# A mixture-of-experts layer on one core: layer 3's cross terms, its gives and the W3 split behind layer 2's second near bank

## The chip, the cores and the metric

The kernel runs on one core of one Trainium2 chip. The metric is the device time of one execution in microseconds (us); lower is better. Engines: PE (TensorE, matmuls; PEld its weight loads), DVE (VectorE), ACT (ScalarE), POOL (GpSimd) and SP (SyncE, DMA issue).

## The reference

Each of 64 x 64 = 4096 tokens has 256 features. A gate picks two of eight experts for a token; each expert is a network of three layers (256 to 512 to 512 to 256), and the two results, weighted, are added to the token.

```python
gate = xn @ wg_W + wg_b + (genre_embed @ gg_W + gg_b)      # xn: x, RMS-normed
gate_w = softmax(gate); topk_w, topk_i = top_k(gate_w, 2)
cw = sum(one_hot(topk_i, 8) * topk_w[..., None])           # 8 weights, 6 of them 0
h1 = relu(einsum('bsh,ehm->bsem', x, W1) + b1)
h2 = relu(einsum('bsem,emn->bsen', h1, W2) + b2)
out_e = einsum('bsen,enh->bseh', h2, W3) + b3
return x + einsum('bseh,bse->bsh', out_e, cw)
```

## The kernel before

The tokens are routed on the chip: each expert's tokens are gathered into tiles of up to 128, run through the three layers, and added back to their rows in DRAM. The first part of the tokens gives the units 0 to 5 (one tile each, plain fp32 matmuls) while the routing of the rest is computed. From unit F = 6 a unit has 2 to 4 tiles of one expert, up to 512 tokens wide, and `row(u)` writes one unit. Which of 40 shapes the rest has is known at run time; a switch jumps to the code of that shape. In the execution profiled there are units 6 to 24, in groups of two or three units of one expert: 6-8, 9-11, 12-14, 15-16, 17-18, 19-20, 21-22, 23-24. Their widths are 384 columns but for 8 (480), 9 (352), 12 (312), 15 (504), 16 (512), 18 (400), 21 (344) and 24 (320).

In these units each fp32 operand is split into a high and a low part (`h`, `l`) and their spread (`d`), on ACT (high) and DVE (low, spread), and each product is taken in two passes:

- `near(u, l, n)`: high x high and low x low into PSUM bank n (0 to 3), line 1100, and then ACT scales the bank in place and adds the bias (line 1108). One call is a "near bank": 8 matmuls in layer 2, 4 in layer 1.
- `cross(u, l, n)`: the spreads' product is added to the same bank (line 1115), and then ACT writes the ReLU's high part (`h1h`, line 1124, or `h2h`, 1127) and DVE the low part (`h1l`, `h2l`, 1140).

Layer 3 of unit u - 1 runs inside `row(u)`. `near3` (1189) sums high and low products into banks 5 and 6, `scale3` (DVE, 1203) scales them in place and adds the bias, `cross3` (1209) adds the spreads' product, and `give` (ACT, 1232) multiplies each tile's rows with the token's weight into a buffer `ysE` or `ysO`, from which POOL adds them to the rows in DRAM (line 1251, an indirect DMA that must find the adds of the unit before landed). `spans` (1085) make `h1d` and `h2d`.

The last unit of a group also splits the next expert's weights: W1 (`high_w` on ACT as `w1h`, `low_w` and `span_w` on DVE), then W2 in two halves (`w2h`, line 1039, two ACT instructions of 1.05 us). The first unit of a group splits its W3 (`w3h` on ACT, `w3l` on DVE). `split_rows` (ACT `xh`, line 1075; DVE `xl`, 1076) splits the next unit's tokens.

The order on each engine is the order in which the code is written (`tc.manual_schedule()`): each engine takes its instructions in this order and waits on semaphores where data is not ready. In a unit PE's order is: four near banks and four cross banks of layer 1, `near3`, the first near bank of layer 2, `cross3`, three near banks, four cross banks.

Of the kernel before, what the change touches and what calls it, by code (L numbers as in the profile page):

```python
# [68 lines left out]
def kernel(  # L69
# [92 lines left out]
    w1l = [wall.tile([P, HC, M], F32R, name=f"w1{a}") for a in "hld"]  # L162
# [609 lines left out]
    ww, ex, cgs = {}, {}, {}  # L772
# [36 lines left out]
    def width(u):  # L809
        return BT if u < F else WQ * plan[u - F][1]  # L810
# [4 lines left out]
    def follow(u):  # L815
        return u > F and group(u) == group(u - 1)

    def size(u):
        return (width(u) + BT - 1) // BT
# [48 lines left out]
    def gather_cw(u):  # L868
        for k, b in enumerate(tiles(u)):
            cg = cgs[b] = cgR[:, u % NCG, k]  # L870
            fetch(cg, (cwdA if b < F else cwdR)[:, :], b)
# [27 lines left out]
    def transpose_x(u, which=None):  # L899
        bs, w, s0 = tiles(u), len(tiles(u)), slots(u).start  # L900
        if u > F:
            for k in range(w) if which is None else which:
                V.transpose(
                    xT[:, :, s0 + k, :].rearrange("p c (b k) -> p k c b", b=SQ),
                    shs[:, s0 + k].rearrange("p k (a c) -> p k c a", a=SQ),
                )
            return
        tp = PB[4][:, 0 : HC * BT].rearrange("p (c t) -> p c t", c=HC)
        g = ring(run, [P, H], "xg", 3, bs[0]).rearrange("p (r c) -> p c r", c=HC)
        for c in range(HC):  # L910
            nc.tensor.transpose(tp[:, c], g[:, c], ident)
        nc.scalar.copy(xT[:, :, s0, :], tp)
# [38 lines left out]
    def streams(u, end):  # L951
        q = mybir.EngineType.SP
        if F < u + 1 < end and not follow(u + 1):
            stream_3(u + 1, q)
        if F < u + 2 < end and not follow(u + 2):
            stream_1(u + 2, q)
            stream_2(u + 2, q)

    def stage_1(u):

        if u < F:
            ww[u] = [w1r[u % RING], vT[:, :, u, :], w2r[u % RING], w3r[u % RING]]
            return
        if follow(u):
            ex[u] = ex[u - 1]
            ww[u] = ww[u - 1][0:4]
            return
        e = ex[u] = expert(u, mybir.EngineType.DVE)
        bb = ring(run, [P, 2, MC], "bb", 3, group(u))
        V.tensor_copy(bb.unsqueeze(2), vT[:, :, e])  # L970
        k = group(u) % RING
        ww[u] = [w1r[k], bb, w2r[k], w3r[k]]

    def scales(u):

        n = size(u)
        cw = ring(run, [P, SLOTS], "cw", 3, u)
        V.tensor_copy(cw[:, 0:n].unsqueeze(2), cgR[:, u % NCG, 0:n, ex[u]])
        for k, b in enumerate(tiles(u)):
            cgs[b] = cw[:, k : k + 1]  # L980

    def scaled(u, eng="V"):
        for _ in scaling(u, eng):
            pass
# [50 lines left out]
    def plain(t):  # L1035
        return t.bitcast(F32)

    def high_w(dst, src):
        nc.scalar.activation(dst[0], src, AF.Copy, scale=NEAR * FINE)

    def low_w(dst, src):
        V.scalar_tensor_tensor(dst[1], plain(dst[0]), -1.0 / FINE, src, ALU.mult, ALU.add)

    def span_w(dst):
        V.tensor_tensor(dst[2], plain(dst[0]), plain(dst[1]), ALU.subtract)
# [16 lines left out]
    def w2_of(u, n, m):  # L1062
        cs = slice(n * P, m * P)
        return [t[:, :, cs] for t in room["w2"]], ww[u][2][:, :, cs]
# [17 lines left out]
    def spans(t3, u):  # L1082

        h, l, d = (t[:, :, 0 : width(u)] for t in t3)
        V.scalar_tensor_tensor(d, plain(l), 1.0 / FINE, plain(h), ALU.mult, ALU.subtract)  # L1085

    def fine(u, last):

        return u >= F and size(u) > 1 and u + 1 < last
# [4 lines left out]
    def near(u, l, n):  # L1094

        ws, xs = (w1l, xl) if l == 0 else (room["w2"], room["h1"])
        bank, k = PB[n][:, 0 : width(u)], HC if l == 0 else MC
        for c in range(k):
            for t in (0, 1):
                nc.tensor.matmul(  # L1100
                    bank,
                    lhsT=ws[t][:, c, ts(n, P)],
                    rhs=xs[t][:, c, 0 : width(u)],
                    start=c == 0 and t == 0,
                    stop=c == k - 1 and t == 1,
                    skip_group_check=True,
                )
        nc.scalar.activation(bank, bank, AF.Identity, bias=ww[u][1][:, l, n : n + 1], scale=1.0 + 1.0 / FINE)  # L1108
# [89 lines left out]
    def scale3(u):  # L1198
        row = b3_sb[:, ex.pop(u)]
        for k in range(0, size(u), 2):  # L1200
            n = min(2, size(u) - k)
            two = PB[5 + k // 2][:, 0 : n * H].rearrange("p (k h) -> p k h", k=n)
            V.scalar_tensor_tensor(two, two, 1.0 + 1.0 / FINE, row.to_broadcast([P, n, H]), ALU.mult, ALU.add)
# [41 lines left out]
    def pay():  # L1245
        adds.append([])
        add_rows(*owed.pop(0))
# [93 lines left out]
    def fetches_of(u, last):  # L1341
        far = F + 1 < u + 2 < last
        if far:
            gather_unit(u + 2)
            stow(u + 2)
        return far
# [26 lines left out]
    def row(u, last):  # L1373

        streams(u, last)
        far = fetches_of(u, last)
        if u == F:
            gather_cw(F)
            pay()
        follows = u + 1 < last  # L1380
        fresh_next = follows and not follow(u + 1)
        if follows:
            gather_cw(u + 1)
        n3, limbs = size(u - 1), fine(u - 1, last)
        fresh = u > F and not follow(u)
        if u == F + 1:
            scales(F)
        third = fine(u, last) and not (follow(u) and fine(u - 1, last))
        if third and not limbs:
            high_w(room["w3"], ww[u][3])  # L1390
        for n in range(MC):
            near(u, 0, n)
        if limbs:
            spans(room["h2"], u - 1)
            if not follow(u - 1):
                span_w(room["w3"])
        if fresh and not limbs:
            for n in (0, 2):
                span_w(w2_of(u, n, n + 2)[0])
        if third and not limbs:  # L1400
            low_w(room["w3"], ww[u][3])
        if follows and u > F:
            stage_1(u + 1)
            if u > F + 1 and not (fresh and limbs):
                transpose_x(u + 1)
        for n in range(MC):
            cross(u, 0, n)
        if fresh_next:
            high_w(w1l, ww[u + 1][0])
        if limbs:  # L1410
            near3(u - 1)
            if fresh and follows:
                transpose_x(u + 1, (0, 1))
            scale3(u - 1)
            if fresh and follows:
                transpose_x(u + 1, range(2, size(u + 1)))
        else:
            scaled(u - 1, "A")
            layer3(u - 1)
        if u == F:  # L1420
            split_w(*w2_of(u, 2, 4))
            stage_1(u + 1)
        if u == F + 1:
            transpose_x(u + 1)
        if fresh and limbs:
            for n in (0, 2):
                span_w(w2_of(u, n, n + 2)[0])
        spans(room["h1"], u)
        if u == F:
            transpose_x(u + 1)  # L1430
        else:
            scales(u)
        if far:
            shuffle(u + 2)
        near(u, 1, 0)
        if limbs:
            cross3(u - 1)
        give(u - 1)
        if third and limbs:
            high_w(room["w3"], ww[u][3])  # L1440
            low_w(room["w3"], ww[u][3])
        if fresh_next:
            low_w(w1l, ww[u + 1][0])
            span_w(w1l)
        near(u, 1, 1)
        if u == F:
            near(u, 1, 2)
            near(u, 1, 3)
        if follows:
            split_rows(u + 1)  # L1450
        elif not fine(u, last):
            scaled(u, "A")
        if fresh_next:
            high_w(*w2_of(u + 1, 0, 2))
            low_w(*w2_of(u + 1, 0, 2))
        if u > F:
            near(u, 1, 2)
            near(u, 1, 3)
        if fresh_next:
            high_w(*w2_of(u + 1, 2, 4))  # L1460
        for n in range(MC):
            cross(u, 1, n)
            if n == MC - 1 and follows:
                span_rows(u + 1)
            if n == 2 and hints:
                hints.pop()()
        if fresh_next:
            low_w(*w2_of(u + 1, 2, 4))
# [103 lines left out]
```

## Time and profile before

| | |
|---|---|
| time, median of 3 runs | 419.32 us (419.04 to 419.55) |
| the profiled execution: its own time, its span | 422.99 us, 421.3 us |
| granted TensorE clock in it | 0.997 |
| PE, PEld, DVE, ACT, POOL busy | 97%, 91%, 84%, 62%, 73% of the span |
| units 6 to 24 | from 74.6 us to the end; the last matmul starts at about 415 us |

A profile is one execution, and every duration below is from it. A line of a timeline gives the start, the duration, the engine and source line, output<-inputs, the shapes, how many instructions are merged ("x3"), and in brackets the idle time before them and what ended it. A line of a group gives its instructions' busy time and mean, and behind the second bar the idle time before them and its releasers. Matmuls overlap and their ends are modelled, so distances between matmuls are taken from start to start: 0.17 us at 384 columns, 0.12 us at 256.

### The profile page before, as it was taken

The page shows a single profiled execution, that of the slowest core. Times are in us where ns is not written, and L with a number is a line of the kernel's source. Part 1 is how long each engine was busy: PE and PEld are TensorE (multiplying, and loading weights), DVE is VectorE, ACT ScalarE, POOL GpSimd, SP SyncE. Part 2 cuts the span into 40 slices and gives each one's busy share as a digit, 9 for nine tenths or more (in the row PEclk, how much of TensorE's full clock was granted, in tenths as well). Part 3 has the DMA queues.
Part 4 walks back from the last instruction along what each step waited for, and adds up shares of the span by engine and source line. Part 5 has one row for each costly group of instructions (what it writes and reads, how often), then busy time and mean ns, then how long its engine had stood idle before and what let it go on. Part 6 is the DMA issues. An engine that isn't in the chain of part 4 may idle for free.

```text
span 421.3 us, 7909 instructions
## 1 busy us (share of the span) xinstructions
PE 408.8 (97%) x2664; PEld 385.1 (91%) x2664; DVE 351.9 (84%) x613; ACT 262.4 (62%) x536; POOL 306.8 (73%) x239
## 2 busy tenths in 40 slices
PE   8999999999999999999999999999999999999994
PEld 6788999799989999999999889899999989999992
DVE  5887986898879987899598979799988979989931
ACT  5965635764765748658468565748566575675750
POOL 6257347768888888878778888888788787874544
PEclk9999999999999999999999999999999999999998
DMA  8899996898735666538557663927386385550323
GB/s 309 304 331 386 379 370 185 232 260 248 165 76 112 177 161 150 115 87 228 140 141 208 158 125 91 259 71 136 93 240 148 76 212 160 106 105 8 39 29 44
DMA packets 72052, 72.31 MB, mean 172 GB/s; under 512 B 36191, under 2 KB 59074, under 8 KB 71620
## 3 DMA queue, kind: packets, MB, share of 16 engines
q1 hardware_dynamic: 56640, 54.04, 39.5%
q0 software_dynamic: 15008, 17.68, 23.5%
q8 instruction: 22, 0.36, 0.4%
q14 instruction: 26, 0.21, 0.2%
q10 hardware_dynamic: 356, 0.01, 0.0%
HBM read 55.86 MB, written 20.47 MB: 181 GB/s over the span
## 4 chain that ended last, share of the span: by engine, by line
PE 79%; DVE 5%; issue 5%; DMA 3%; POOL 3%; POOLq 2%; ACT 1%; SPq 0%; DVEq 0%; ACTq 0%
PE pb L1100 34%; PE pb L1115 16%; PE pb L1189 11%; PE pb L1209 6%; PE pb L1026 4%; DMA big<-in_x_dram 3%; PE pb L1014 2%; PE pb L1176 2%; POOL out_dram L1251 2%; POOLq L1487 1%; PE pb L272 1%; POOL cg L846 1%; DMA out_dram<-ysO,idxR 1%; PE pb L646 1%; DVE h2l L1140 1%
## 5 line engine op out<-in xcount | busy, mean ns | idle before, releaser
L1108 ACT ACTIVATE pb<-pb,bb 128x384 f32<-128x384 f32 (+8 forms) x152 | 84.8, 560 | 96.0 <-PE pb L1100 77.5
L1100 PE MATMUL pb<-h1h,w2h 128*128 128x384 f32 (+8 forms) x304 | 102.8, 340 | 0.0
L1100 PE MATMUL pb<-h1l,w2l 128*128 128x384 f32 (+8 forms) x304 | 102.8, 340 | 0.0
L846 POOL DMA_INDIRECT cg<-cwdR,idxR x61 | 77.6, 1272 | 18.6 <-issue 16.5
L1251 POOL DMA_INDIRECT out_dram<-ysE,idxR x30 | 58.9, 1962 | 16.2 <-ACT ysE L1232 8.9
L1251 POOL DMA_INDIRECT out_dram<-ysO,idxR x28 | 47.6, 1702 | 18.5 <-ACT ysO L1232 11.5
L1100 PEld LDWEIGHTS pb<-h1l,w2l 128*128 128x128 f32 x304 | 57.2, 188 | 2.3 <-DVE h1l L1140 0.2
L1100 PEld LDWEIGHTS pb<-h1h,w2h 128*128 128x128 f32 x304 | 57.2, 188 | 1.6
L1115 PE MATMUL pb<-h1d,w2d 128*128 128x384 f32 (+8 forms) x304 | 57.2, 339 | 0.2 <-ACT pb L1108 0.2
L1140 DVE SCALAR_TENSOR_TENSOR h2l<-pb,h2h 128x384 fp32r<-128x384 f32 (+7 forms) x72 | 39.2, 567 | 21.0 <-ACT h2h L1127 13.9
L1189 PE MATMUL pb<-w3l,h2l 128*128 128x256 f32 (+5 forms) x232 | 56.1, 282 | 0.0
L1189 PE MATMUL pb<-w3h,h2h 128*128 128x256 f32 (+5 forms) x232 | 56.1, 282 | 0.0
L1115 PEld LDWEIGHTS pb<-h1d,w2d 128*128 128x128 f32 x304 | 52.4, 188 | 2.2 <-ACT pb L1108 0.5
L1100 PE MATMUL pb<-xh,w1h 128*128 128x384 f32 (+8 forms) x152 | 51.8, 343 | 1.1 <-DVE h2l L1140 0.8
L1100 PE MATMUL pb<-xl,w1l 128*128 128x384 f32 (+8 forms) x152 | 51.3, 339 | 0.0
L846 POOL DMA_INDIRECT xgE<-in_x_dram,idxR x33 | 43.4, 1315 | 10.1 <-issue 7.9
L846 POOL DMA_INDIRECT xgO<-in_x_dram,idxR x28 | 37.5, 1340 | 8.5 <-issue 8.2
L1189 PEld LDWEIGHTS pb<-w3l,h2l 128*128 128x128 f32 (+5 forms) x232 | 43.3, 187 | 0.2
L1189 PEld LDWEIGHTS pb<-w3h,h2h 128*128 128x128 f32 (+5 forms) x232 | 43.3, 187 | 0.2
L1127 ACT ACTIVATE h2h<-pb 128x384 fp32r<-128x384 f32 (+7 forms) x72 | 34.4, 503 | 9.3 <-PE pb L1115 8.0
L1140 DVE SCALAR_TENSOR_TENSOR h1l<-pb,h1h 128x384 fp32r<-128x384 f32 (+8 forms) x76 | 37.5, 555 | 0.9 <-ACT h1h L1124 0.9
L1085 DVE SCALAR_TENSOR_TENSOR h1d<-h1l,h1h 128x1536 fp32r<-128x1536 f32 (+8 forms) x19 | 33.8, 1781 | 0.0
(278 smaller groups left out, 799.8 us busy)
## 6 DMA issues: line engine op xcount, KB each, us to landing
w2r<-in_L_cond_W_dram SPq DMA_DIRECT2D x14, 1024.0 KB
w1r<-in_L_cond_W_dram SPq DMA_DIRECT2D x14, 512.0 KB
w3r<-in_L_cond_W_dram SPq DMA_DIRECT2D x14, 512.0 KB
gTs<-scr SPq DMA_DIRECT2D x13, 384.0 KB
out_dram<-in_x_dram SPq DMA_DIRECT2D x4, 768.0 KB
scr<-xgO SPq DMA_DIRECT2D x7, 384.0 KB
scr<-xgE SPq DMA_DIRECT2D x6, 384.0 KB
big<-in_x_dram SPq DMA_DIRECT2D x4, 512.0 KB
```

Source lines behind the costliest of these rows:

```text
L846: return nc.gpsimd.indirect_dma_start(out=dst, out_offset=None, in_=src, in_offset=bass.IndirectOffsetOnAxis(ap=index(b), axis=0), bounds_ ...
L1014: nc.tensor.matmul(ph, lhsT=w1[:, c, ts(m, P)], rhs=cols[:, c, :], start=(c == 0), stop=(c == HC - 1))
L1026: nc.tensor.matmul(ph, lhsT=w2[:, m, ts(n, P)], rhs=hid[0][:, m], start=(m == 0), stop=(m == MC - 1))
L1085: V.scalar_tensor_tensor(d, plain(l), 1.0 / FINE, plain(h), ALU.mult, ALU.subtract)
L1100: nc.tensor.matmul(bank, lhsT=ws[t][:, c, ts(n, P)], rhs=xs[t][:, c, 0 : width(u)], start=c == 0 and t == 0, stop=c == k - 1 and t == 1, s ...
L1108: nc.scalar.activation(bank, bank, AF.Identity, bias=ww[u][1][:, l, n : n + 1], scale=1.0 + 1.0 / FINE)
L1115: nc.tensor.matmul(bank, lhsT=ws[2][:, c, ts(n, P)], rhs=xs[2][:, c, 0 : width(u)], start=False, stop=c == k - 1, skip_group_check=True,)
L1127: nc.scalar.activation(room["h2"][0][:, n, 0 : width(u)], bank, AF.Relu, scale=NEAR)
L1140: V.scalar_tensor_tensor(l, PB[n][:, 0 : width(u)], 0.0, plain(h), ALU.max, ALU.subtract)
L1189: nc.tensor.matmul(sums(u, k)[0 : cols.stop - cols.start], lhsT=room["h2"][t][:, n, cols], rhs=room["w3"][t][:, n, :], start=n == 0 and t ...
L1209: nc.tensor.matmul(sums(u, k)[0 : cols.stop - cols.start], lhsT=room["h2"][2][:, n, cols], rhs=room["w3"][2][:, n, :], start=False, stop=n ...
L1251: add = nc.gpsimd.indirect_dma_start(out=orows, out_offset=bass.IndirectOffsetOnAxis(ap=index(b)[0 : y.shape[0]], axis=0), in_=y, in_offse ...
```

## The change

In `row(u)` the second near bank of layer 2 moves ahead of `cross3`, the gives and the split of W3. The split of the next W1 (`low_w`, `span_w`, on DVE) moves with it. Nothing is added or removed.

```diff
         near(u, 1, 0)
+        if fresh_next:
+            low_w(w1l, ww[u + 1][0])
+            span_w(w1l)
+        near(u, 1, 1)
         if limbs:
             cross3(u - 1)
         give(u - 1)
         if third and limbs:
             high_w(room["w3"], ww[u][3])
             low_w(room["w3"], ww[u][3])
-        if fresh_next:
-            low_w(w1l, ww[u + 1][0])
-            span_w(w1l)
-        near(u, 1, 1)
```

`limbs` holds where unit u - 1 is split (from u = 7), `third` in a group's first unit, `fresh_next` in its last.

On PE, in unit 8 (480 columns), banks 68, 69 and 70 are layer 2's first, second and third near bank, and 73 and 74 the banks of layer 3; the rows with - are where `cross3` stood, those with + where it stands now, with the second near bank between them:

```order
 L1100 MATMUL pb_68<-h1l,w2l 128x480
-L1209 MATMUL pb_73<-w3d,h2d 128x256 x8
-L1209 MATMUL pb_74<-w3d,h2d 128x256 x4
 L1100 MATMUL pb_69<-h1h,w2h 128x480
 L1100 MATMUL pb_69<-h1l,w2l 128x480
+L1209 MATMUL pb_73<-w3d,h2d 128x256 x8
+L1209 MATMUL pb_74<-w3d,h2d 128x256 x4
 L1100 MATMUL pb_70<-h1h,w2h 128x480
```

`cross3` stands 8 matmuls later, in every unit from 7 to 24.

On ACT, in unit 11, the last of its group (384 columns; `w2h` are the halves of the next expert's W2):

```order
 L1108 ACTIVATE pb_68<-pb_68,bb_934 128x384
+L1108 ACTIVATE pb_69<-pb_69,bb_934 128x384
 L1232 ACTIVATE ysE<-pb_73,cw_1300 128x256 x2
 L1232 ACTIVATE ysE<-pb_74,cw_1300 128x256
-L1108 ACTIVATE pb_69<-pb_69,bb_934 128x384
 L1075 ACTIVATE xh<-xT 128x2x312
 L1039 ACTIVATE w2h<-w2r_86 128x4x256
```

The second bank's scaling now precedes the three gives; `xh` follows them directly.

On ACT, in unit 12, the first of its group (312 columns):

```order
 L1108 ACTIVATE pb_68<-pb_68,bb_935 128x312
+L1108 ACTIVATE pb_69<-pb_69,bb_935 128x312
 L1232 ACTIVATE ysO<-pb_73,cw_1301 128x256 x2
 L1232 ACTIVATE ysO<-pb_74,cw_1301 128x256
 L1039 ACTIVATE w3h<-w3r_89 128x1024
-L1108 ACTIVATE pb_69<-pb_69,bb_935 128x312
 L1075 ACTIVATE xh<-xT 128x2x384
```

Here the W3 split goes behind the second bank's scaling too. On DVE, POOL and SP the order of these units is unchanged.

## The prediction

> **What bounds the kernel now.** I read the page's busy shares and chain first, then the groups by line and the waits of the weight loads, then the timelines of PE, VectorE (DVE), ScalarE (ACT) and POOL around layer 2's first near bank.
>
> ```profile
> PE 408.8 (97%) x2664; PEld 385.1 (91%) x2664; DVE 351.9 (84%) x613; ACT 262.4 (62%) x536; POOL 306.8 (73%) x239
> PE 79%; DVE 5%; issue 5%; DMA 3%; POOL 3%; POOLq 2%; ACT 1%; SPq 0%; DVEq 0%; ACTq 0%
> ```
>
> PE is busy for 97% of the span and makes 79% of the chain that ended last. The change moves no work from one engine to another, so what it can give is PE's idle time near the moved instructions.
>
> ```profile
> L1209 PE MATMUL pb<-w3d,h2d 128*128 128x256 f32 (+5 forms) x232 | 31.5, 286 | 1.2 <-issue 0.7 <-DVE pb L1203 0.4
> L1209 PEld LDWEIGHTS pb<-w3d,h2d 128*128 128x128 f32 (+5 forms) x232 | 28.8, 186 | 3.7 <-issue 2.0 <-DVE pb L1203 1.2
> ```
>
> L1209 is `cross3`. Its weight loads (PEld) stood 3.7 us idle, of which the row names 3.2: 2.0 "issue" and 1.2 for L1203, VectorE's `scale3`. The matmuls themselves show only 1.2, because the pipelined end of the matmul before covers the start of a wait. Matmul starts tell more. First a unit that waits, then one that does not (both PE):
>
> ```profile
> 153.46 0.39 PE L1100 MATMUL pb<-h1l,w2l 128*128 128x384 f32 x1
> 154.02 1.68 PE L1209 MATMUL pb<-w3d,h2d 128*128 128x256 f32 x12 [0.17 <-issue]
> 155.54 0.34 PE L1100 MATMUL pb<-h1h,w2h 128*128 128x384 f32 x1
> ...
> 402.44 0.31 PE L1100 MATMUL pb<-h1l,w2l 128*128 128x320 f32 x1
> 402.58 1.60 PE L1209 MATMUL pb<-w3d,h2d 128*128 128x256 f32 x12
> 404.02 0.31 PE L1100 MATMUL pb<-h1h,w2h 128*128 128x320 f32 x1
> ```
>
> In the first, `cross3` starts 0.56 us after the last near matmul, in the second 0.14; and it then takes 1.52 instead of 1.44 until the next group starts. So one wait costs PE about 0.5. VectorE's timeline says what is late:
>
> ```profile
> 151.43 1.92 DVE L1140 SCALAR_TENSOR_TENSOR h1l<-pb,h1h 128x384 fp32r<-128x384 f32 x4
> 153.28 1.02 DVE L1203 SCALAR_TENSOR_TENSOR pb<-pb,b_sb 128x512 f32<-128x512 f32 x2
> 154.21 1.73 DVE L1085 SCALAR_TENSOR_TENSOR h1d<-h1l,h1h 128x1536 fp32r<-128x1536 f32 x1
> 155.87 0.14 DVE L978 COPY cw<-cg 128x3 f32 x1
> 159.07 0.96 DVE L1076 TENSOR_TENSOR xl<-xT,xh 128x768 fp32r<-128x768 f32 x1 [3.06 <-ACT pb L1108]
> ```
>
> `scale3` follows four `h1l` on a queue without a gap; its first bank ends just before 154.02, where `cross3` starts. By 156.0 VectorE is idle, for 3.06 us. It is late at this one place and ahead after it.
>
> **The change part by part.** *The waits of `cross3`.* Behind the second near bank `cross3` comes one bank later, 1.39 us at 384 columns (eight steps of 0.17), far more than 0.5, so `scale3` is done. The second near bank needs nothing new: all four `h1l` were read by the first. What is late next is `h1d`, needed by layer 2's cross terms: it ends at 155.94, and those start four near banks and `cross3` after 152.2, past 159. The gain lies between 1.2 (the matmul row) and 3.7 (the weight loads' row). Starts as above agree with the upper end; I take 3.4.
>
> *ScalarE in a group's last unit.* There the next expert's W2 is split, and ACT is full to the end (ACT, then the two rows of DVE and PE that follow from it):
>
> ```profile
> 171.13 0.56 ACT L1108 ACTIVATE pb<-pb,bb 128x384 f32<-128x384 f32 x1 [2.60 <-PE pb L1100]
> 172.55 1.21 ACT L1232 ACTIVATE ysE<-pb,cw 128x256 f32<-128x256 f32 x3 [0.87 <-PE pb L1209]
> 173.95 0.56 ACT L1108 ACTIVATE pb<-pb,bb 128x384 f32<-128x384 f32 x1 [0.19 <-issue]
> 174.43 0.72 ACT L1075 ACTIVATE xh<-xT 128x624 fp32r<-128x624 f32 x1
> 175.04 1.05 ACT L1039 ACTIVATE w2h<-w2r 128x1024 fp32r<-128x1024 f32 x1
> 175.99 0.54 ACT L1108 ACTIVATE pb<-pb,bb 128x384 f32<-128x384 f32 x1
> 176.72 0.56 ACT L1108 ACTIVATE pb<-pb,bb 128x384 f32<-128x384 f32 x1 [0.19 <-PE pb L1100]
> 177.20 1.05 ACT L1039 ACTIVATE w2h<-w2r 128x1024 fp32r<-128x1024 f32 x1
> 178.15 1.24 ACT L1127 ACTIVATE h2h<-pb 128x384 fp32r<-128x384 f32 x3
> ...
> 178.66 1.98 DVE L1140 SCALAR_TENSOR_TENSOR h2l<-pb,h2h 128x384 fp32r<-128x384 f32 x4 [1.31 <-ACT w2h L1039]
> ...
> 179.30 0.39 PE L1100 MATMUL pb<-xh,w1h 128*128 128x312 f32 x1
> ```
>
> The next unit's first matmul at 179.30 overwrites bank 0, so it needs the first `h2l`, which (a quarter of 1.98 after 178.66) ended only 0.1 before: lateness on ACT here goes straight to PE. Until now the gives (L1232) ran while PE did the second near bank. Now they start 1.39 later, at 173.94, take 1.10 until the next can start, and `xh` goes from 174.43 to 175.04. From there the steps of these rows run on: `w2h` 175.65, L1108 176.60 and 177.07, against 176.72 now, where it waited for PE. That is 0.35 late. But this give started 1.6 after its `cross3`, others 1.2 (in the last unit 403.74, quoted below, against 402.58): with that 0.4 back nothing is late. So 0 to 0.45 (a wider `xh` adds 0.1) in each of the five last units of 384 or 400 columns, 0 to 2.3; units of 480 and 512 have near banks long enough to hide it. I take 0.2 each, 1.0, as the two starts are about equally common. In a group's first unit the split of W3 goes behind the gives in the same way, and no W2 split follows:
>
> ```profile
> 354.13 1.21 ACT L1232 ACTIVATE ysE<-pb,cw 128x256 f32<-128x256 f32 x3 [0.78 <-PE pb L1209]
> 355.22 1.07 ACT L1039 ACTIVATE w3h<-w3r 128x1024 fp32r<-128x1024 f32 x1
> ...
> 358.40 0.52 ACT L1108 ACTIVATE pb<-pb,bb 128x344 f32<-128x344 f32 x1 [0.53 <-PE pb L1100]
> ```
>
> Gives at 355.4 (a bank of 344 columns is 1.25), `w3h` at 356.5, `xh` at 357.4, then L1108 at 358.1 and 358.6: 0.2 late where ACT had 0.53 to spare, and made good by the `h2h` that follow. Nothing. `low_w`, `span_w` of W1 keep their place on VectorE, since neither near banks nor gives run there; SP's order stays too.
>
> The rule that speaks against the change is the Trainium skill's (TensorE: Matmul & The Clock Gate, Architectural detail): ScalarE's queue is a strict FIFO, so a give that waits holds all behind it. The rows agree: ACT's order stood through every wait above. By the rule alone, with no give starting early, the toll would be its upper end, 2.3, and the sum -0.6.
>
> *POOL.* The scatter-adds keep their order but wait for later gives. Inside the run they push the gathers behind them, whose rows VectorE transposes (L903); that never waits now:
>
> ```profile
> L903 DVE STREAM_TRANSPOSE xT<-gTs 128x256 f32<-128x256 f32 x58 | 31.4, 631 | 0.0
> ```
>
> The gathers run a unit ahead, so 1.4 is hidden there. At the end it shows:
>
> ```profile
> 403.74 1.21 ACT L1232 ACTIVATE ysO<-pb,cw 128x256 f32<-128x256 f32 x3 [0.46 <-PE pb L1209]
> ...
> 404.50 1.55 POOL L1251 DMA_INDIRECT out_dram<-ysO,idxR  x1 [8.82 <-ACT ysO L1232]
> ...
> 408.19 3.65 DMA out_dram<-ysO,idxR
> ...
> 411.82 0.48 DVE L1234 SCALAR_TENSOR_TENSOR xg<-pb,cw,bc 128x256 f32<-128x256 f32 x1 [7.92 <-PE pb L1176]
> ...
> 412.71 1.54 POOL L1251 DMA_INDIRECT out_dram<-xg,idxR  x1 [2.97 <-DVE xg L1234]
> 414.76 1.55 POOL L1251 DMA_INDIRECT out_dram<-xg,idxR  x1 [0.51 <-DVE xg L1234]
> 416.61 1.44 POOL L1251 DMA_INDIRECT out_dram<-xg,idxR  x1 [0.30 <-issue]
> ```
>
> The last three adds may start only when the three before have landed, now at 408.19 + 3.65 = 411.84, before their give ends at 412.30. In the last unit nothing waited, so its `cross3` moves by one near bank, 402.58 - 401.41 = 1.17, and the landing to 413.0. The first add then starts 0.4 later, at 413.4, the others at POOL's step of 1.85: the third at 417.1 instead of 416.61. That is 0.5 lost; from 0.2 (if the landing is quicker) to 0.8.
>
> *A stall of the profiled run.* In one last unit ACT stood 1.67 us before L1108, and PE paid later:
>
> ```profile
> 339.50 0.56 ACT L1108 ACTIVATE pb<-pb,bb 128x384 f32<-128x384 f32 x1 [1.67 <-PE pb L1100]
> ...
> 342.19 1.67 PE L1115 MATMUL pb<-h1d,w2d 128*128 128x384 f32 x8 [0.18 <-ACT pb L1108]
> 344.61 0.43 PE L1100 MATMUL pb<-xh,w1h 128*128 128x344 f32 x1 [0.76 <-DVE h2l L1140]
> ```
>
> The change puts that L1108 ahead of the gives; 0 to 0.9 (0.18 + 0.76) could go. I count 0, since nothing in the order explains the stall.
>
> **Sum**: -3.4 + 1.0 + 0.5 = -1.9 us. The profiled execution took 422.99 (span 421.3); the median of the runs is 419.32, 0.9% less, and I take the same microseconds off it: 417.4. Ends: -3.7 - 0.9 + 0.2 = -4.4, or 414.9, and -1.2 + 2.3 + 0.8 = +1.9, or 421.2.
>
> **Rivals.** *The whole gain* (0.17): gives start early everywhere and the stall goes with them: -3.4 - 0.9 + 0.5 = -3.8, 415.5. For it: three of the seven last units have 0.5 us waits whose removal leaves ACT time; against: the stall has no cause that the change touches.
>
> *The wait moves* (0.21): VectorE sets the pace of the waiting units, and what `cross3` no longer waits for is waited for at `h2l` or the next `h1l`. Then two thirds of 3.4 come back: -1.1 + 1.0 + 0.5 = +0.4, 419.7, no change. Against it stand the 3.06 us in which VectorE waited for ACT in such a unit.
>
> *Slower* (0.12): ACT's order. If gives and what follows are late by 0.9 instead of 0.2 in the five units, as after the 1.67 at 339.50, then -3.4 + 4.5 + 0.5 = +1.6, 420.9. It decides from (3.4 - 0.5 + 0.84) / 5 = 0.75 a unit, twice what the rows of 171 to 179 give at worst. The FIFO rule above is its ground.
>
> **How the numbers follow.** The forecast has 0.50, the rivals 0.17, 0.21 and 0.12. About 0.2%, or 0.84 us, is what can be told from no change here, 418.5 to 420.2. The forecast (416.5 to 418.6 by itself) and the whole gain make faster, less a little of the forecast's upper side: 0.66. The moved wait and that side make 0.23 for the same, the slow rival 0.11. The range from 415.3 to 419.7 leaves out the slow rival and a part of the whole gain.
>
> **What would show it.** Right: idle before L1209's weight loads under 0.5 us; gives starting after a second near bank; the first matmul of the units after a W2 split idle by 0.2 more; the last unit's adds 1.2 nearer to the final ones. Wrong: new idle of PE before L1115 or at a unit's first L1100 of over 2 us in sum, or waits of `cross3` that stay.

## The result and the profile after

The changed kernel took 421.31 us (median of 19 runs, 419.79 to 423.9) against 419.1 us before (19 runs, 418.26 to 421.76): ratio 1.0052, interval 1.0036 to 1.0067, so it is 0.5% slower. The prediction was 417.4, faster. The profiled execution took 421.01 us, its span is 419.3, its granted clock 0.991. Ratios here leave out runs in a slower state of the chip and are not the quotient of the two medians.

The waits of `cross3` are gone. The two rows of L1209 in the changed kernel, matmuls and weight loads, show next to no idle time (1.2 and 3.7 us before):

```profile
L1209 PE MATMUL pb<-w3d,h2d 128*128 128x256 f32 (+5 forms) x232 | 30.5, 282 | 0.0
L1209 PEld LDWEIGHTS pb<-w3d,h2d 128*128 128x128 f32 (+5 forms) x232 | 29.5, 185 | 0.3
```

A new wait stands in the page of the changed kernel: the busy line, the chain, the group of near matmuls, and the transposes, which never waited before.

```profile
PE 407.0 (97%) x2664; PEld 386.6 (92%) x2664; DVE 351.2 (84%) x613; ACT 261.9 (62%) x536; POOL 314.8 (75%) x239
...
PE 81%; DVE 6%; DMA 5%; issue 3%; ACT 2%; POOL 1%; POOLq 1%; SPq 0%; DVEq 0%; ACTq 0%
...
L1100 PE MATMUL pb<-h1h,w2h 128*128 128x384 f32 (+8 forms) x304 | 104.0, 344 | 2.4 <-DVE h1l L1140 2.4
...
L903 DVE STREAM_TRANSPOSE xT<-gTs 128x256 f32<-128x256 f32 x58 | 31.3, 629 | 3.3 <-DMA gTs<-scr 3.3
```

All of it is in one place. PE's timeline of the changed kernel at unit 14 (start, duration; the last matmul of `near3`, then layer 2's first near bank), and below it the same time in stretches (length, busy time of PE, PEld, DVE, ACT and POOL, then the granted clock, DMA share and GB/s):

```profile
214.53 0.28 PE L1189 MATMUL pb<-w3l,h2l 128*128 128x256 f32 x1
217.24 0.69 PE L1100 MATMUL pb<-h1h,w2h 128*128 128x384 f32 x1 [2.43 <-DVE h1l L1140]
217.73 0.53 PE L1100 MATMUL pb<-h1l,w2l 128*128 128x384 f32 x1
218.05 0.53 PE L1100 MATMUL pb<-h1h,w2h 128*128 128x384 f32 x1
```

```profile
208.00:217.00 9.00, 6.81 (x47) 6.61 (x45) 5.60 (x10) 5.06 (x10) 7.47 (x6) 1.00 0.91 212
217.00:219.00 2.00, 1.76 (x5) 1.76 (x6) 2.00 (x5) 0.00 (x0) 1.39 (x3) 0.50 0.26 78
219.00:222.00 3.00, 3.00 (x16) 3.00 (x16) 3.00 (x5) 0.80 (x2) 2.70 (x2) 0.77 0.40 97
```

From start to start 2.71 us pass instead of 0.12: a gap of 2.59. Behind it the clock is 0.50, and matmuls of 384 columns follow each other at 0.32 us instead of 0.17 until about 220.4. The same two matmuls before:

```profile
218.54 0.28 PE L1189 MATMUL pb<-w3l,h2l 128*128 128x256 f32 x1
218.66 0.34 PE L1100 MATMUL pb<-h1h,w2h 128*128 128x384 f32 x1
```

This is not the profiled run alone. The granted clock is 0.991 or 0.992 in 16 of the 19 runs; in the other three it is 0.994 to 0.996, and they are the three fastest (419.79, 420.17 and 420.65 us). Half clock for 3.4 us, as in the profile, lowers the mean clock of 419 us by about 0.004.

What PE waited for is the rows of unit 15. GpSimd gathers them in unit 13, SP writes them to DRAM (`scr<-xgO`) and reads them back shuffled (`gTs<-scr`), and VectorE transposes them in unit 14, ahead of `h1l`. Before, from the timelines of POOL (first and last of the four gathers) and SP, with VectorE's row at the end:

```profile
196.56 1.07 POOL L846 DMA_INDIRECT xgO<-in_x_dram,idxR  x1 [0.30 <-issue]
...
200.59 1.00 POOL L846 DMA_INDIRECT xgO<-in_x_dram,idxR  x1 [0.30 <-issue]
...
203.48 0.37 SPq L886 DMA_DIRECT2D scr<-xgO  x1
207.58 0.37 SPq L894 DMA_DIRECT2D gTs<-scr  x1
...
215.47 2.08 DVE L903 STREAM_TRANSPOSE xT<-gTs 128x256 f32<-128x256 f32 x4
```

After:

```profile
197.03 1.07 POOL L846 DMA_INDIRECT xgO<-in_x_dram,idxR  x1 [0.30 <-issue]
...
202.36 1.00 POOL L846 DMA_INDIRECT xgO<-in_x_dram,idxR  x1 [0.30 <-issue]
...
205.99 0.37 SPq L886 DMA_DIRECT2D scr<-xgO  x1
209.91 0.37 SPq L894 DMA_DIRECT2D gTs<-scr  x1
...
214.81 1.99 DVE L903 STREAM_TRANSPOSE xT<-gTs 128x256 f32<-128x256 f32 x4 [3.26 <-DMA gTs<-scr]
```

Layer 2 of unit 13 starts at 201.63 before and 197.85 after. Counted from there, the last gather starts at -1.04 before and 4.51 after, and the read-back at 5.95 and 12.06: 6.1 later. With the landing time of after (214.81 - 209.91 = 4.9) the rows would have been there at 212.5 before, 3.0 ahead of VectorE's use at 215.47. VectorE is 0.14 earlier in its unit after (215.47 - 201.63 = 13.84 before, 214.81 - 3.26 - 197.85 = 13.70 after), and 6.1 - 3.0 + 0.14 is the 3.26 that it waited.

The head of the program, up to unit 7, varies from run to run by more than the change is worth (in the profiles below unit 7's second layer starts between 95 and 105 us). So stretches are compared, from the start of one unit's first layer 2 matmul to that of another, read from PE's timeline of each profiled run, one for each kernel:

| kernel | 9 to 16 | gap at 14 | 16 to 24 | 24 to end of span | 7 to end |
|---|---|---|---|---|---|
| before | 122.94 | 0 | 142.92 | 19.89 | 323.07 |
| after | 126.12 | 2.59 | 139.66 | 20.95 | 324.05 |
| e0, before again | 122.96 | 0 | 143.76 | 19.81 | 324.12 |
| e1, old order in 9 to 13 | 123.68 | 0 | 139.69 | 20.80 | 321.49 |
| e2, new order in 9 to 13 | 125.87 | 1.89 | 142.36 | 19.88 | 325.54 |
| e3, after, transposes behind | 123.50 | 0 | 139.17 | 20.77 | 320.75 |
| e4, before, transposes behind | 122.16 | 0 | 139.67 | 19.79 | 318.94 |
| e5, after, gathers first | 122.05 | 0 | 139.72 | 21.12 | 320.20 |
| e6, before, more POOL work | 129.62 | 5.02 | 141.50 | 19.99 | 328.50 |
| e7, after, gap filled | 125.02 | 0.3 | 139.68 | 21.39 | 323.40 |
| e8, e3 with last unit old | 122.01 | 0 | 139.24 | 21.19 | 319.76 |
| e9, e4 again | 123.22 | 0 | 141.10 | 19.79 | 321.42 |
| e10, after, last unit old | 125.91 | 2.21 | 139.66 | 19.84 | 322.73 |
| e11, after, spreads in four | 122.65 | 0 | 140.39 | 20.97 | 322.71 |

Units 7 to 9 take 37.3 to 37.6 in all but e11 (38.7). For the same reason a time is compared only with that of before measured beside it: 427.4 us (median) beside e0 to e3, 418.85 beside e4 to e7, 424.2 beside e8 and e9, and 420.0 (one run) beside e10 and e11. The times not given below are medians of 426.88 (e1), 430.19 (e2) and 425.50 (e3), and 425.69 (e6), 420.86 (e7) and 420.18 (e10) in one run each.

### The profile page after: what moved, and what is told of

Read it like the earlier page. It is cut to its first block, busy times and chain, and to the rows that moved or that the text cites. A ratio compares the mean times of both kernels' runs of the same rounds, so it can differ in the third digit from the quotient of the medians.

```text
span 419.3 us, 7909 instructions
## 1 busy us (share of the span) xinstructions
PE 407.0 (97%) x2664; PEld 386.6 (92%) x2664; DVE 351.2 (84%) x613; ACT 261.9 (62%) x536; POOL 314.8 (75%) x239
## 4 chain that ended last, share of the span: by engine, by line
PE 81%; DVE 6%; DMA 5%; issue 3%; ACT 2%; POOL 1%; POOLq 1%; SPq 0%; DVEq 0%; ACTq 0%
PE pb L1100 36%; PE pb L1115 17%; PE pb L1189 12%; PE pb L1209 6%; PE pb L1026 3%; PE pb L1176 3%; DMA big<-in_x_dram 2%; PE pb L1014 2%; DVE sqV L263 2%; DMA gTs<-scr 1%; PE pb L646 1%; DMA scr<-xgO 1%; DMA xgO<-in_x_dram,idxR 1%; DVE xT L903 1%; POOLq L1567 1%
## 5 line engine op out<-in xcount | busy, mean ns | idle before, releaser
L1100 PE MATMUL pb<-h1h,w2h 128*128 128x384 f32 (+8 forms) x304 | 104.0, 344 | 2.4 <-DVE h1l L1140 2.4
L846 POOL DMA_INDIRECT cg<-cwdR,idxR x61 | 83.7, 1371 | 18.6 <-issue 16.2
L1251 POOL DMA_INDIRECT out_dram<-ysE,idxR x30 | 60.0, 2000 | 9.4 <-issue 3.4
L1251 POOL DMA_INDIRECT out_dram<-ysO,idxR x28 | 50.5, 1805 | 17.6 <-ACT ysO L1232 9.7
L846 POOL DMA_INDIRECT xgE<-in_x_dram,idxR x33 | 43.6, 1323 | 10.2 <-issue 9.5
L846 POOL DMA_INDIRECT xgO<-in_x_dram,idxR x28 | 36.4, 1301 | 8.5 <-issue 7.9
L1140 DVE SCALAR_TENSOR_TENSOR h1l<-pb,h1h 128x384 fp32r<-128x384 f32 (+8 forms) x76 | 37.6, 558 | 0.0
L903 DVE STREAM_TRANSPOSE xT<-gTs 128x256 f32<-128x256 f32 x58 | 31.3, 629 | 3.3 <-DMA gTs<-scr 3.3
```

Of the source, the lines that this page charges most:

```text
L846: return nc.gpsimd.indirect_dma_start(out=dst, out_offset=None, in_=src, in_offset=bass.IndirectOffsetOnAxis(ap=index(b), axis=0), bounds_ ...
L903: V.transpose(xT[:, :, s0 + k, :].rearrange("p c (b k) -> p k c b", b=SQ), shs[:, s0 + k].rearrange("p k (a c) -> p k c a", a=SQ),)
L1100: nc.tensor.matmul(bank, lhsT=ws[t][:, c, ts(n, P)], rhs=xs[t][:, c, 0 : width(u)], start=c == 0 and t == 0, stop=c == k - 1 and t == 1, s ...
L1140: V.scalar_tensor_tensor(l, PB[n][:, 0 : width(u)], 0.0, plain(h), ALU.max, ALU.subtract)
L1251: add = nc.gpsimd.indirect_dma_start(out=orows, out_offset=bass.IndirectOffsetOnAxis(ap=index(b)[0 : y.shape[0]], axis=0), in_=y, in_offse ...
```

## The experiments

**e0: a second profile of before.** No edit.

> The kernel before once more, for a second profile of it. The first profile took 422.99 us, 3.7 above the median of its runs, and its layer 2 of unit 7 began at 98.23 us against 95.25 with the change. Queue theory (GpSimd runs without a pause from unit 9 on and holds the row gathers back): the head's 3 us are chance, since GpSimd and TensorE shift together there; in this profile unit 7 begins at 95 to 96, the transposes of unit 15's rows (in unit 13) still wait for nothing, and the time is 418.5 to 419.5. Rival (the early TensorE alone, not the change, makes the gathers late): with unit 7 at 95 the transposes wait here too, by 1 to 3 us.

It took 427.59 us. Its head is slower still (unit 7 at 101.58, not 95), which leaves that part of the expectation untested here (other runs test it, below), but unit 9 to 16 is as before, 122.96. What moved is unit 20: 19.46 us, after 18.61 in the first profile.

**e1 and e2: which units make the loss.** The new order stands only where `ahead` is false; e1 has `ahead = 9 <= u <= 13`, e2 the reverse.

```diff
         near(u, 1, 0)
+        ahead = 9 <= u <= 13
...
-        near(u, 1, 1)
+        if not ahead:
+            near(u, 1, 1)
         if limbs:
             cross3(u - 1)
...
+        if ahead:
+            near(u, 1, 1)
```

> The changed kernel with the old order in units 9 to 13. Queue theory: GpSimd falls behind in units 9 to 13 because the gives come 1.4 us later there; with the old order there the gathers of unit 15's rows are in time, the 2.6 us gap at unit 14 and the 1.6 us of halved clock behind it are gone, the gains in units 18 and 20 to 23 (about 1.2 to 2.5) stay, and the end stays 1.1 later: 417.3 to 418.8, that is 2.5 to 4 below the changed kernel. Rival (ScalarE's FIFO in the five last units): only unit 11's toll goes, 0.2 to 0.5, so 420.8 to 421.1. Rival (the clock drops by itself): clock stays at 0.991 and the time near 421.3.

Ratio to before 0.9978 (0.9952 to 1.0005). No gap at 14; 9 to 16 is 123.68, of which 0.71 is a pause in unit 11 that before did not have. The second half keeps its gain.

> The kernel before with the new order in units 9 to 13 alone. Queue theory: the gap at unit 14 is there, 2 to 3 us with 1.6 of halved clock behind, the waits removed in units 10 to 13 give 0.6 to 0.9, the end costs nothing: 419.1 + 4.2 - 0.8 = 422.5 (421.5 to 423), slower than the changed kernel. Rival (ScalarE's FIFO): one of five tolls, 419.0 to 419.5, the same as before.

Ratio 0.9997 (0.9952 to 1.0042), which decides nothing and misses the expected 422.5. The stretches do: 2.93 lost from 9 to 16, the rest as before. The gap is 1.89 of it; in the same unit, shortly ahead of the gap, PE lost another 1.16 waiting for ScalarE. The loss is made in units 9 to 13, not by ScalarE in the last units of all groups.

**e3 and e4: VectorE's transposes out of the way.** In e3 (on the changed kernel) and e4 (on the kernel before):

```diff
         if follows and u > F:
             stage_1(u + 1)
-            if u > F + 1 and not (fresh and limbs):
-                transpose_x(u + 1)
+        behind = follows and u > F + 1 and not (fresh and limbs)
...
             scale3(u - 1)
+            if behind:
+                transpose_x(u + 1)
```

> The changed kernel; on VectorE the transposes of the next unit's rows stand behind the layer 3 scaling instead of ahead of the low parts of layer 1, in all units that are not first of a group. Queue theory: the rows still arrive late for unit 15, but TensorE no longer waits for that: gap and halved clock gone, 421.3 - 4.2 = 417.1 (416.3 to 418.3). Rival (the wait moves): the rows' high part and so unit 15's first matmul are late by as much as the rows, 2 us or more of TensorE idle there, 419 to 421. Rival (ScalarE's FIFO): no change, 421.3.

Ratio 0.9963 (0.9924 to 1.0003). The gap is gone, and the wait did not move: unit 15 takes 21.58, as everywhere. A pause of 1.5 us fell into unit 11.

> The kernel before, with only VectorE's order changed: the transposes of the next unit's rows behind the layer 3 scaling, in units that are not first of a group. Both the waits of cross3 and the pressure on the gathers come from VectorE's queue by the queue theory: the scaling then starts 1.6 us earlier, the waits of cross3 in units 10, 13, 18, 20 and 21 to 23 shrink without moving cross3 and the gives. From unit 9 to unit 16 TensorE takes 122.0 to 122.6 us (122.94 before, 126.12 with the change), from unit 16 to the end 160.5 to 162 (162.8 before), and the end is not later. In all 1 to 2.5 below before. Rival (the spreads of layer 1 become late instead, since VectorE does them behind the transposes): second-layer cross terms wait, 0.5 us or more in each unit, and nothing is won. Rival (ScalarE's FIFO made the change slow): no statement on this one, same as before.

416.18 us against 418.85, ratio 0.9958 (0.9930 to 0.9986): faster. From unit 16 to the end it took 159.46, a microsecond less than expected. The weight loads of `cross3` in e4 wait 1.7 us instead of 3.7, without `cross3` having moved:

```profile
L1209 PEld LDWEIGHTS pb<-w3d,h2d 128*128 128x128 f32 (+5 forms) x232 | 29.2, 185 | 1.7 <-DVE pb L1203 1.2
```

**e5 and e6: GpSimd's order and load.** e5 puts a unit's scatter-adds on a list when they are given, and issues them in the next unit behind its row gathers:

```diff
         far = fetches_of(u, last)
+        settle()                       # issues the adds on the list
...
-        give(u - 1)
+        give(u - 1, defer=u > F + 1 and u + 3 < last)
```

> The changed kernel; on GpSimd the scatter-adds of a unit are issued one unit later, behind the next row gathers (from unit 8 to the last unit that still gathers). Queue theory: the gathers no longer stand behind three adds of about 5.7 us, unit 15's rows come 4 us or more earlier, and the gap and the halved clock at unit 14 are gone: unit 9 to unit 16 takes 122.0 to 123 us (126.12 with the change), unit 16 to the end 160 to 161.5 as with the change. Rival (GpSimd is short of time as such and its order doesn't matter: the debt goes to the adds, and gives wait for a free buffer): a gap of over 1 us in some unit from 14 on, at a give or at cross3, and 124 or more. Rival (ScalarE's FIFO): 126, as with the change.

417.12 us against 418.85, ratio 0.9952 (0.9935 to 0.9969): faster. PE's work is that of the changed kernel; only GpSimd's order differs. e6 does the opposite to the kernel before:

```diff
         if follows:
             gather_cw(u + 1)
+        if 10 <= u <= 12:
+            for v in (u + 1, u + 4):
+                fetch(cgR[:, v % NCG, SLOTS - 1], cwdR[:, :], tiles(u)[0])
```

> The kernel before with GpSimd delayed: six more gathers of one token tile's weights into unused slots, two each in units 10, 11 and 12, about 1.3 us each with 0.3 between (9.6 in all, of which its 2 us of idle time hide a part). TensorE's order is that of before. Queue theory: GpSimd is late by 5 to 8 us at unit 15's gathers, as with the change, TensorE waits 1.5 to 4 us before unit 14's second layer with 1.6 of halved clock behind it, and unit 9 to unit 16 takes 125 to 128 us instead of 122.94. Rival (ScalarE's FIFO or the place of cross3 itself makes the loss): 122.9 to 123.5.

With the old order and a busier GpSimd the same wait appears, larger than expected: 129.62 from 9 to 16. The two groups of e6 and PE at unit 14:

```profile
L1100 PE MATMUL pb<-h1h,w2h 128*128 128x384 f32 (+8 forms) x304 | 103.7, 343 | 4.9 <-DVE h1l L1140 4.9
...
L903 DVE STREAM_TRANSPOSE xT<-gTs 128x256 f32<-128x256 f32 x58 | 31.4, 630 | 7.1 <-DMA gTs<-scr 7.1
```

```profile
221.06 0.64 PE L1100 MATMUL pb<-h1h,w2h 128*128 128x384 f32 x1 [4.86 <-DVE h1l L1140]
221.49 0.53 PE L1100 MATMUL pb<-h1l,w2l 128*128 128x384 f32 x1
```

**e7: the clock behind the gap.** 20 matmuls into bank 4, which nothing else uses there:

```diff
+        if u == 14:
+            for k in range(20):
+                nc.tensor.matmul(PB[4][0:BT, 0:H], lhsT=room["h2"][0][:, 0, 0:BT],
+                                 rhs=room["w3"][0][:, 0, :], start=True, stop=True)
         near(u, 1, 0)
```

> The changed kernel with 20 more matmuls (128 x 256, 0.12 us each, 2.4 us in all, result unused) ahead of the second layer of unit 14, where TensorE stood 2.59 us. Clock theory: the halved clock behind the gap (steps of 0.32 instead of 0.17 us for ten matmuls) is a result of the pause; with the pause filled the steps stay at 0.17, the granted clock of the run at 0.996 or more, and unit 13's to unit 15's begin takes 37.5 to 37.8 us instead of 39.26. Rival (the throttle is due to something else at this point): steps of 0.32 remain and 39.2.

PE's timeline of e7, and the stretch (columns as above):

```profile
215.11 2.56 PE L1437 MATMUL pb<-w3h,h2h 128*128 128x256 f32 x20
217.83 0.44 PE L1100 MATMUL pb<-h1h,w2h 128*128 128x384 f32 x1 [0.16 <-DVE h1l L1140]
218.12 0.34 PE L1100 MATMUL pb<-h1l,w2l 128*128 128x384 f32 x1
218.29 0.34 PE L1100 MATMUL pb<-h1h,w2h 128*128 128x384 f32 x1
```

```profile
217.00:219.00 2.00, 1.84 (x12) 1.53 (x11) 2.00 (x5) 0.00 (x0) 1.53 (x2) 1.00 0.41 132
```

The step is 0.17 again and the clock 1.00; units 13 and 14 take 38.15 instead of 39.26. That is 1.1 won, 0.4 less than the halved clock cost, as layer 2 of unit 14 began 0.14 later than in the changed kernel and a few steps were 0.23 to 0.29.

**e8 and e9: the two edits together, and e4 again.** e8 is e3 with `ahead = u + 1 == last`.

> The changed kernel with VectorE's transposes behind the layer 3 scaling, and the old order in the last unit alone. Queue theory, from the stretches measured so far: unit 7 to 9 takes 37.3 us, 9 to 16 takes 122.0 (123.50 in the run with the last unit in the new order, less a stall of 1.5 in unit 11 that no other run had), 16 to 24 takes 139.2, and the end 19.8 instead of 20.8 to 21.0, since the last adds of unit 23 land 1.2 us sooner. Sum 318.3 against 318.94 of the kernel before with the transposes moved: 0.2 to 0.9 us faster than that one in the same call, and 2.5 to 4 faster than before. Rival (the end is set by the last matmuls and its own adds, not by unit 23's adds): the end stays at 20.8 or more.

> The kernel before with the transposes moved behind the layer 3 scaling, once more, for a comparison with the version above on one chip. All theories: the same stretches as the first time (122.2 from unit 9 to 16, 139.7 to unit 24, 19.8 to the end) and 2 to 3.5 us below before. Unit 20 takes 16.5 again, without the pause of 1 to 2 us that it had in three of the kernels with the old order; if the pause was chance, it may come back here.

e8: 421.41 us against 424.18, ratio 0.9933 (0.9898 to 0.9968), the lowest ratio of all; e9: 422.69, ratio 0.9958 (0.9925 to 0.9992). Both beat before; between the two the runs do not decide. Two things missed. The pause in unit 20 came back in e9 (17.86), with others in 13 and 14, so it is not bound to the place of the transposes. Over all profiles it goes with the head: apart from the gap at 14, pauses of 0.7 us or more from unit 9 on stand in six of the seven profiles in which unit 7's second layer begins later than 98 us (before, e0 to e3 and e9; not e8), in kernels of both orders, and in none of the seven in which it begins before 96. And e8's end stayed at 21.19, though its gives were early. What held it, as far as the profile shows, is a drain of GpSimd ahead of the last unit's adds. Its row in e8 (duration least, median and greatest in ns, first and last start), then POOL's last add of unit 22 and first of unit 23:

```profile
L1495 POOLq DRAIN  x1: 13919/13919/13919, 387.6 to 387.6; - x1
```

```profile
393.81 1.55 POOL L1251 DMA_INDIRECT out_dram<-ysE,idxR  x1 [0.31 <-ACT pb L1108]
402.49 1.55 POOL L1251 DMA_INDIRECT out_dram<-ysO,idxR  x1 [7.13 <-ACT ysO L1232]
```

The drain ends at 401.5, 6.2 us after that last add was issued (395.36). The profile names the give as releaser; it had been done for more than a microsecond.

**e10: the end alone.** The changed kernel with `ahead = u + 1 == last`.

> The changed kernel with the old order in the last unit alone, for the end: with the change it lasts 20.95 us from unit 24's second layer on, before 19.89; with the transposes moved and the old order in the last unit it was still 21.19, there with unit 23's adds at 4.28 us behind a drain of GpSimd that ended at 3.36. Theory (the later of two sets the end: the gives, or the drain, which ends 6.1 to 6.2 us after unit 22's last add): with the change the drain ends at 1.37, so the old order's gives at 2.3 count again, the adds start at 3.1 and the end is 19.8 to 20.0. Rival (the gives don't matter and the end follows GpSimd's debt alone): 20.8 or more. The gap at unit 14 stays in both (2.5 to 2.7 us).

The end is 19.84, as the drain theory had it; the gap at 14 is 2.21, less than the 2.5 to 2.7 expected. GpSimd in the last unit of after, then of e10 (layer 2 of unit 24 starts at 398.35 and 398.56):

```profile
402.60 1.55 POOL L1251 DMA_INDIRECT out_dram<-ysO,idxR  x1 [9.04 <-ACT ysO L1232]
...
411.07 1.54 POOL L1251 DMA_INDIRECT out_dram<-xg,idxR  x1 [3.22 <-DMA out_dram<-ysO,idxR]
...
414.77 1.44 POOL L1251 DMA_INDIRECT out_dram<-xg,idxR  x1 [0.30 <-issue]
```

```profile
401.64 1.55 POOL L1251 DMA_INDIRECT out_dram<-ysO,idxR  x1 [7.86 <-ACT ysO L1232]
...
410.05 1.54 POOL L1251 DMA_INDIRECT out_dram<-xg,idxR  x1 [3.16 <-DVE xg L1234]
...
413.76 1.44 POOL L1251 DMA_INDIRECT out_dram<-xg,idxR  x1 [0.30 <-issue]
```

In after the last three adds wait for the landing, in e10 for VectorE.

**e11: why GpSimd is slow.** Each spread as four instructions, one for each block of 128 features:

```diff
-        V.scalar_tensor_tensor(d, plain(l), 1.0 / FINE, plain(h), ALU.mult, ALU.subtract)
+        for n in range(MC):
+            V.scalar_tensor_tensor(d[:, n], plain(l)[:, n], 1.0 / FINE, plain(h)[:, n], ...)
```

> The changed kernel with each spread of layer 1's and 2's activations (h1d, h2d, one VectorE instruction of up to 1536 columns and 1.7 us) in four instructions of a quarter each. Theory (GpSimd's DMA steps wait while a VectorE instruction with two SBUF inputs runs, so a gather beside h1d takes 2.21 us in the mean and up to 3.04 instead of 1.0): beside a quarter it waits a quarter, the gathers there take 1.5 or less in the mean, GpSimd's busy time falls from 314.8 to 305 to 311, and the gap at unit 14 is 0 to 2 us instead of 2.59. Rival (the VectorE queue keeps the way closed through back-to-back instructions): gathers of 2 to 3 us stay and the gap too. Rival (the long gathers come from something else, such as DMA traffic): no change.

GpSimd's busy time fell by 29.5 us, far more than expected, and no gap is left at unit 14. The busy line of e11, the weight gathers of after and of e11 (busy, mean ns):

```profile
PE 406.2 (97%) x2664; PEld 384.7 (92%) x2664; DVE 358.4 (86%) x724; ACT 262.0 (63%) x536; POOL 285.3 (68%) x239
```

```profile
L846 POOL DMA_INDIRECT cg<-cwdR,idxR x61 | 83.7, 1371 | 18.6 <-issue 16.2
```

```profile
L846 POOL DMA_INDIRECT cg<-cwdR,idxR x61 | 66.7, 1094 | 18.6 <-issue 15.2
```

Its time in one run, 419.5 against 419.99, says little; a new wait for rows (2.71 us on VectorE) in unit 7 cost it 1.4.

## Why the prediction was wrong

*The waits of `cross3`* (-3.4): right in kind, a little large. Set unit by unit against before, units 9, 10, 12, 13, 17, 18 and 20 to 23 lost 0.05, 0.47, 0.28, 0.22, 0.03, 0.47, 0.43, 0.34, 0.46 and 0.12 us, in all 2.87 (unit 13 by its 16.81 in e3, e5 and e8, unit 20 against its 17.20 in e6, where neither kernel paused).

*ScalarE in a group's last unit* (+1.0): too dear. Unit 14 without the gap is 18.35 (e1, e5) instead of 18.24; in the others the toll is within the figures above, since each became shorter or stayed. The gives start early: in units 9 to 24 of the changed kernel each begins 1.14 to 1.16 after its `cross3`. In unit 11, where it was 1.6 before, it is 1.15 (PE and ACT of the changed kernel):

```profile
168.81 1.59 PE L1209 MATMUL pb<-w3d,h2d 128*128 128x256 f32 x12
...
169.96 1.21 ACT L1232 ACTIVATE ysE<-pb,cw 128x256 f32<-128x256 f32 x3 [0.39 <-PE pb L1209]
```

So the waits and ScalarE together are -2.76, against -2.4 in the sum. That these are near is in part luck: the gain was 0.5 too large and the toll 0.9 too dear. The rival by ScalarE's order falls with this and with e5, where ScalarE's order is that of the change and the loss is gone; its 420.9 is the nearest to the measured time, but its mechanism cost 0.11, not 4.5.

*POOL, "the gathers run a unit ahead, so 1.4 is hidden there"*: this step failed. A unit ahead was true of the order, not of the time: the rows landed only some 3.0 us before they were used. Nor was the delay the 1.4 of the later gives, as the expectation of e1 still had it. The adds waited less for gives than before, as the page's rows of before and of after show (mean ns, idle time and its main releaser):

```profile
L1251 POOL DMA_INDIRECT out_dram<-ysE,idxR x30 | 58.9, 1962 | 16.2 <-ACT ysE L1232 8.9
```

```profile
L1251 POOL DMA_INDIRECT out_dram<-ysE,idxR x30 | 60.0, 2000 | 9.4 <-issue 3.4
```

In this part GpSimd has no pause; it sets its own pace. Its 31 steps from unit 9's first add to the first gather of unit 15's rows, before and after (length, busy time):

```profile
140.10:196.56 56.46, 46.88 (x31) 1.00 0.59 146
```

```profile
137.13:197.03 59.90, 50.45 (x31) 1.00 0.60 149
```

The rest, 9.6 and 9.5 us, is the 0.3 between two steps: the same. The steps themselves took 3.57 longer (the gathers among them 1.46, the adds 2.11), the whole stretch 3.44, and PE was 0.8 us ahead by its own gain in units 9 to 12. Together that is the 4.25 by which the first of these gathers was late for unit 13 (196.56 - 201.63 against 197.03 - 197.85). Of the 6.1 of the read-back, 1.30 more are lost from the first to the last of the four gathers (5.33 us instead of 4.03), the rest behind them. Why the steps are longer, e11 shows in part: they stretch beside long VectorE instructions. Of the 95 gathers of the middle part before and 92 after (L846, from 92 to 350 us), those that started while no VectorE instruction with two SBUF inputs ran (54 and 56) took 1.03 and 1.04 us in the mean; those that started beside `h1d` or `h2d` took 1.98 before (21) and 2.25 after (19), and those beside another such instruction 1.45 (20 and 17). The change shifts GpSimd against VectorE, and in this part it met more of these: 14 of the 31 steps before and 16 after started beside one, and took 26.50 and 31.29 us, the others 20.38 and 19.16. That this shift makes the whole 3.57 is an inference; that the debt of GpSimd makes the gap is shown by e5, e6 and e11.

The rival in the expectation of e0, that the early head and not the change makes the gathers late, does not fit the profiles. The first of the gathers starts 0.81 to 0.83 us before layer 2 of unit 13 in the six with the new order in units 9 to 13 and GpSimd's order and the spreads as they were (after, e2, e3, e7, e8 and e10; unit 7 at 95 to 103 us), and 5.07 before it in the three with the old order and nothing else changed there (before, e0 and e1; 98 to 105 us). The order is not all that counts, though: with the transposes moved, the old order gave 5.06 in e9 but 1.84 in e4, where the 31 steps took 49.72 us. In e4 this costs nothing, since `h1l` no longer stands behind the transposes.

The price of the gap is what the prediction had nowhere: 19.39 - 16.81 = 2.58 in unit 13 and 19.87 - 18.35 = 1.52 of halved clock in unit 14, 4.1 us. Of the signs named ahead, that of being right came (the weight loads of `cross3` idle for 0.3 us); the new idle time of PE came at layer 2's first near bank, for which no sign was named.

*POOL at the end* (+0.5, at most 0.8): right mechanism, too small. It measured 1.06, and e10 takes it back. The landing took 411.07 - 406.30 - 0.3 = 4.5 us in after (0.3 is the step between two issues), where 3.65 was assumed from a row in which it did not bind.

*The stall of the profiled run* (0): it went with the change in that profile, 18.61 - 0.43 - 16.77 = 1.41, but e9 has a pause there too, and such pauses go with a slow head, not with one of the two orders. What causes them was not settled.

The sum from unit 7: -2.76 + 4.10 + 1.06 - 1.41 = +0.99; measured 324.05 - 323.07 = +0.98. Without the pause, +2.40 on 419.1 gives 421.5, and the median is 421.31. That the median run of before has no such pause is an inference: its span, about 417.4 (in both profiles the time is 1.7 more than the span), leaves 95.7 us up to unit 7 without the pause, as in the seven profiles with a fast head (95.1 to 95.8), and 94.3 with it, less than in any profile. The rival "the wait moves" had the right sign, but named VectorE's pace; what VectorE waited for was GpSimd.

## What to carry to other kernels

A transfer that runs a unit ahead has slack in microseconds, and that is measured from its landing to its use, not from the order; an idle time of 0.0 at the user does not tell how near it is. Before anything is made faster, look for an engine that runs without a pause beside the one at the limit: it does not get faster with it, and what it feeds will be late. Here taking the waiting instruction out of the way of the critical one (e4) won more safely than moving the critical one.

## What was not expected of the hardware

A pause of 2.59 us of PE halved its clock for 3.4 us (0.50 over 2.00 us, then 0.77 over 3.00). The gap of 1.89 in e2 did not (granted clock 1.00 behind it), those of 2.21 (e10, 0.70 over 1.80 us and then 0.61 over 3.00) and 5.02 (e6, 0.54 and then 0.61, each over 2.00) did. Worked out from these rows, the half clock lasted 3.4 us each time, however long the gap was. Whether only the length of a gap counts, or also its moment, these four gaps do not show. The Trainium skill (TensorE: Matmul & The Clock Gate, Why this matters for your kernels) asks to avoid idle gaps of more than about 3 us; in these runs 2.2 was enough, and the measurement decides.

A gather of GpSimd takes 1.0 us alone and up to 3.0 beside one long VectorE instruction with two SBUF inputs. In after, POOL and DVE:

```profile
113.76 2.93 POOL L846 DMA_INDIRECT xgE<-in_x_dram,idxR  x1 [0.30 <-issue]
116.99 1.00 POOL L846 DMA_INDIRECT cg<-cwdR,idxR  x1 [0.30 <-issue]
...
113.67 2.14 DVE L1085 SCALAR_TENSOR_TENSOR h1d<-h1l,h1h 128x1920 fp32r<-128x1920 f32 x1
...
117.05 1.23 DVE L1045 TENSOR_TENSOR w1d<-w1h,w1l 128x1024 fp32r<-128x1024 f32 x1
```

The gather began 0.09 after `h1d` and ended 0.88 after it; a later one began 0.06 before `w1d`, which has two SBUF inputs too, and took 1.00. The Trainium skill (SBUF — State Buffer, SBUF: two separate sides) says that VectorE and GpSimd share a pair of ports as an exclusive lock that the first to start holds for its whole instruction, and that a VectorE instruction with two SBUF inputs takes part in it against a GpSimd operation that reads SBUF. Both rows agree, as the gathers take their row numbers from SBUF, and cutting the spreads in four took 29.5 us off GpSimd. One row shows that the recorded starts are not exact enough to decide who was first: a gather at 184.49 in after began 0.01 before `w2d` and still took 2.08.
